# A gated delta-rule layer with a mixture of experts: the last chunk of each head no longer brings its state forward, and the first rows of x of the second output projection are asked for one step later

## The chip, the core and the metric

The kernel runs on one core of a Trainium2 chip. TensorE (PE) multiplies matrices, VectorE (DVE), ScalarE (ACT) and GpSimd (POOL) do the elementwise work, and SyncE (SP) issues most of the transfers between the chip's memory and the core. Each of them works through a queue of its own in order. The metric is the device time of one execution in microseconds (us), the median of several runs.

## The reference, cut to what matters

```python
xn = layernorm(x)                      # x: 2 x 2048 x 512, f32
q, k, v = silu(conv4(xn @ W))          # 16 heads of 128; the convolution runs over 4 tokens
alpha, beta = sigmoid(xn @ Wa + ba), sigmoid(xn @ Wb + bb)
def step(S, inps):                     # one token, one head; S starts at zero
    Sk = einsum('bhvk,bhk->bhv', S, kt)
    S = at * S - bt * ((Sk - vt) * kt) # the state, 128 x 128
    ot = einsum('bhvk,bhk->bhv', S, qt)
    return S, ot
_, o = scan(step, S0, ...)             # the last S is thrown away
attn = (layernorm(o) * ln_w + ln_b) * sigmoid(xn @ Wg) @ Wo
ffn = moe(first 512 tokens of xn)      # 16 experts, 4 per token
out = x + attn + ffn
```

Only the outputs `ot` are returned. The state that the scan ends with is used nowhere.

## The kernel before

**Tiling.** The tokens of a batch are cut into four blocks of 512 and each block into four chunks of 128, so there are 16 chunks (NC). The 16 heads of a batch are worked on two at a time (HG = 2): eight head pairs for each of the two batches, numbered u = 0 to 15. The token-by-token recurrence is done a chunk at a time with 128 x 128 matrices, and only the state S goes from a chunk to the next one of the same head pair, in the dictionary `state[u]`.

**One step of the recurrence.** `recurrence(b)` (L1118) goes over the 128 chunks of a batch. In a step it interleaves `before` of chunk m (operands that need no state: the decayed scores pT, the chunk's inverse matrix inv, k and v turned by the transposes L994 and L995, copied to `kv` at L1003, and `kg`, which is k times a decay, on POOL at L1009), `after` of chunk m - 1 (products with the state: L1041, r at L1045, w at L1052 and L1056, the state's update L1061 and L1068, the outputs L1076 and L1079) and `output` of chunk m - 2 (normalisation, gate, store of `oT` to oT_d at L1116). Among these stand the projections of the next block (`group`, seven half-size products in place of eight, L833), whose inputs `xr` come from xs_d by the loads of L812, the convolution's taps on DVE (L923), key work for later head pairs, the small triangular inverses on POOL (`inverses`, L268 and L271) and, in the first batch, the experts (L1754, L1771).

**What sets the order.** For PE, DVE, ACT and POOL the order is written out by hand: everything runs under `manual_schedule` for these four, and the generators yield at places that `recurrence` steps through. SP's queue is not written by hand. A scheduler with a simulated clock puts the transfers in order when the program is built. Transfers under `high_priority` are put ahead of others that are ready. A transfer on SP waits at the head of the queue until its buffer is free, its source is written and an older transfer on its semaphore has landed, and what stands behind it waits too.

**Buffers near the change.** `kg` has three buffers (the first output projection later keeps two pieces of weights in them), `S` and `kv` two each, the PSUM tag "c" (pq, pw, pss and the transposed output) two banks. `aTf` has two buffers. The keys' matrices go through them (`put_a`, stored to aT_d at L235), and in the second batch, after the last key, the first rows of x for the output projection.

**The output projections.** `out_pairs(b)` multiplies the gated outputs of two chunks at a time by Wo, again with seven products (L1336), and adds x. Before its first products it collects weights and inputs into buffers that the recurrence has finished with, by `stock`, `fetch_heads` and `get_x`, all through `load` (L1300), which is under `high_priority`. In the second batch `recurrence` steps it once in the last block but one (block n1 - 2, chunk 2), and then goes through it in the last four steps and behind them. The code ahead of its first yield runs in the first of these steps.

Of the kernel before, what the change touches and what calls it, by code (L numbers as in the profile page):

```python
# [8 lines left out]
F32 = mybir.dt.float32  # L9
# [7 lines left out]
P = 128  # L17
# [28 lines left out]
def block_kernel(ctx, tc, x, wq, wk, wv, wg, wo, wa, wb, ba, bb, par, consts,  # L46
# [11 lines left out]
    def bank(pool, tag):  # L58
        return pool.tile([P, 512], F32, tag=tag, name=tag)
# [705 lines left out]
    def bcast(a, n):  # L765
        return bass.AP(a.tensor, a.offset, [*a.ap, (0, n)])

    def v3(t):
        return t.rearrange("p (h j) -> p h j", h=HG)
# [187 lines left out]
    def before(n, c):  # L957

        u, blk = blocks[n]
        b = u // NP  # L960
        hs = slice((u % NP) * HG, (u % NP) * HG + HG)
        decs, kt, qt, _, vs, _ = have[n]
        op = ops[n % 2]
        ci, cs = blk * CB + c, slice(c * C, (c + 1) * C)

        inv = invs[(n * CB + c) % len(invs)]
        for g in range(2):
            nc.sync.dma_start(
                out=inv[g * Q:(g + 1) * Q, :, g * Q:(g + 1) * Q],
                in_=X_d[u][1, :, g, ci, :].rearrange("h (j i) -> j h i", i=Q))  # L970


        px = bank(ps_l, "l")
        nc.tensor.matmul(px[:, 0:Q], lhsT=op["a32"][:, c, :], rhs=op["ilo"][:, c, :],
                         start=True, stop=True)

        pk = bank(ps_l, "l")
        for h in range(HG):
            nc.tensor.matmul(pk[:, h * C:(h + 1) * C], lhsT=kt[:, h, cs], rhs=qt[:, h, cs],  # L979
                             start=True, stop=True)  # L980
        yield
        xs = k2.tile([P, Q], F32, tag="xs", name="xs")
        nc.vector.tensor_copy(xs, px[:, 0:Q])
        pT = k2.tile([P, HG, C], F32, tag="pT", name="pT", bufs=3)
        nc.vector.scalar_tensor_tensor(
            pT, v3(pk[:, 0:HW]), D ** -0.5, decs[:, :, c, 1:], ALU.mult, ALU.mult)
        yield

        pz = bank(ps_l, "l")
        nc.tensor.matmul(pz[:, 0:Q], lhsT=op["ihi"][:, c, :], rhs=xs, start=True, stop=True)  # L990

        pkv = bank(ps_l, "l")
        for h in range(HG):
            nc.tensor.transpose(pkv[:, h * D:(h + 1) * D], kt[:, h, cs], ident)  # L994
            nc.tensor.transpose(pkv[:, HW + h * D:HW + (h + 1) * D], vs[h][:, cs], ident)  # L995
        yield
        top, bot = op["top"][:, c, :], op["bot"][:, c, :]
        iT = k2.tile([P, Q], F32, tag="iT", name="iT")
        nc.vector.transpose(iT, pz[:, 0:Q])
        nc.vector.scalar_tensor_tensor(  # L1000
            top[:, 0:Q], pz[:, 0:Q], second[:, 0:1], top[:, 2 * Q:], ALU.mult, ALU.add)
        kv = k2.tile([P, 2, HG, D], F32, tag="kv", name="kv")
        nc.scalar.copy(kv.rearrange("p s h j -> p (s h j)"), pkv)  # L1003
        for h in range(HG):
            r = 64 * h
            nc.scalar.copy(bot[r:r + Q, r + Q:r + 2 * Q], iT[r:r + Q])  # L1006
            nc.gpsimd.tensor_copy(inv[0:Q, h, Q:2 * Q], iT[r + Q:r + 2 * Q])  # L1007
        kg = k2.tile([P, HG, D], F32, tag="kg", name="kg", bufs=3)
        nc.gpsimd.tensor_tensor(kg, kv[:, 0], bcast(gd1[b][:, ci, hs], D), ALU.mult)  # L1009
        yield  # L1010
        px = bank(ps_l, "l")
        nc.tensor.matmul(px[:, 0:C], lhsT=op["a64"][:, c, :], rhs=wide(top[:, 0:64]), start=True, stop=True)  # L1012
        yield
        xs = k2.tile([P, C], F32, tag="xs2", name="xs2")
        nc.scalar.copy(xs, px[:, 0:C])
        for h in range(HG):
            r = slice(64 * h, 64 * h + 64)
            nc.scalar.copy(inv[64:C, h, 64:C], bot[r, r])
        yield
        pz = bank(ps_l, "l")  # L1020
        nc.tensor.matmul(pz[:, 0:C], lhsT=xs, rhs=bot, start=True, stop=True)
        yield
        nc.scalar.copy(inv[0:64, :, 64:C], v3(pz[0:64, 0:C]))
        found[n, c] = (pT, kv, kg, inv)

    def after(n, c):

        u, blk = blocks[n]
        b = u // NP
        h0 = (u % NP) * HG  # L1030
        _, kt, _, qg, _, _ = have[n]
        pT, kv, kg, inv = found.pop((n, c))
        ci, cs = blk * CB + c, slice(c * C, (c + 1) * C)
        S = state.get(u)

        if S is None:
            r = kv[:, 1]
        else:
            pq = bank(ps_c, "c")
            for h in range(HG):  # L1040
                nc.tensor.matmul(pq[:, h * D:(h + 1) * D], lhsT=kt[:, h, cs], rhs=S[:, h, :],  # L1041
                                 start=True, stop=True)
            r = k2.tile([P, HG, D], F32, tag="r", name="r")
            for h in range(HG):
                nc.vector.scalar_tensor_tensor(  # L1045
                    r[:, h, :], pq[:, h * D:(h + 1) * D], gd0[b][:, ci, h0 + h:h0 + h + 1],
                    kv[:, 1, h, :], ALU.mult, ALU.add)
        yield
        yield
        pw = bank(ps_c, "c")  # L1050
        for h in range(HG):
            nc.tensor.matmul(pw[:, h * D:(h + 1) * D], lhsT=inv[:, h, :], rhs=r[:, h, :],  # L1052
                             start=True, stop=True)
        yield
        w = k2.tile([P, HG, D], F32, tag="w", name="w")
        nc.scalar.copy(w, v3(pw[:, 0:HW]))  # L1056
        yield

        pss = bank(ps_c, "c")
        for h in range(HG):  # L1060
            nc.tensor.matmul(pss[:, h * D:(h + 1) * D], lhsT=kg[:, h, :], rhs=w[:, h, :],  # L1061
                             start=True, stop=True)
        S2 = k2.tile([P, HG, D], F32, tag="S", name="S")
        if S is None:
            nc.vector.tensor_copy(S2, v3(pss[:, 0:HW]))
        else:
            for h in range(HG):
                nc.vector.scalar_tensor_tensor(  # L1068
                    S2[:, h, :], S[:, h, :], gtot[b][:, ci, h0 + h:h0 + h + 1],
                    pss[:, h * D:(h + 1) * D], ALU.mult, ALU.add)  # L1070
        state[u] = S2
        yield

        po = bank(ps_o, "o")
        for h in range(HG):
            nc.tensor.matmul(po[:, h * D:(h + 1) * D], lhsT=pT[:, h, :], rhs=w[:, h, :],  # L1076
                             start=True, stop=S is None)
            if S is not None:
                nc.tensor.matmul(po[:, h * D:(h + 1) * D], lhsT=qg[:, h, cs], rhs=S[:, h, :],  # L1079
                                 start=False, stop=True)  # L1080
        yield

        mv = k2.tile([P, HG, 2], F32, tag="mv", name="mv")
        for h in range(HG):
            st = k2.tile([P, 6], F32, tag="st", name="st")
            nc.vector.bn_stats(st, po[:, h * D:(h + 1) * D])
            nc.vector.bn_aggr(mv[:, h, :], st)
        rs = k2.tile([P, HG], F32, tag="rs", name="rs")
        nc.vector.tensor_scalar(rs, mv[:, :, 1], EPS, None, ALU.add)
        nb = k2.tile([P, HG], F32, tag="nb", name="nb")  # L1090
        nc.vector.tensor_scalar(nb, mv[:, :, 0], -1.0, None, ALU.mult)  # L1091
        nc.gpsimd.tensor_tensor(rs, rs, mhalf[:, 0:HG], ALU.pow)  # L1092
        nc.gpsimd.tensor_tensor(nb, nb, rs, ALU.mult)  # L1093
        outs[n, c] = (po, nb, rs)
# [197 lines left out]
    def out_pairs(b):  # L1292
# [63 lines left out]
        def get_x(i, m, n):  # L1356
            if whole[i % 2]:
                if n == 0:
                    c = 2 * order[i] + m
                    load(whole[i % 2][m], x[b, c * C:(c + 1) * C, :])  # L1360
                return
            load(xs[i % 2][m, n], x[of(i, m, n)])

        def rows(i, *tiles):
            for m, t in enumerate(tiles):
                whole[i][m] = t
                for n in range(2):
                    xs[i][m, n] = t[:, n * TH:(n + 1) * TH]
# [113 lines left out]
        else:  # L1482
# [12 lines left out]
            fetch_heads(a21, 0, 1, 0), fetch_heads(a22[0], 0, 1, 1)  # L1495
            for tag in ("wq", "wv"):
                stock("T2", bp.tile([P, 4 * TH], F32, tag=tag, name="wo", bufs=1), 4)
            rows(0, *(ap.tile([P, HID], F32, tag="aTf", name="xf", bufs=2) for _ in range(2)))
            for m in range(2):
                get_x(0, m, 0)  # L1500
            stock("T1", k2.tile([P, HID], F32, tag="act", name="wo", bufs=1), 2)
            for tag in ("swk", "swq"):
                stock("T1", k2.tile([P, 3 * TH], F32, tag=tag, name="wo", bufs=1), 3)
# [12 lines left out]
            both(s3, a11, a21, ALU.subtract)  # L1516
            e1 = snap(y, 1)
            yield
            rows(1, *(cvp.tile([P, HID], F32, tag="raw", name="xf") for _ in range(2)))
        def late():  # L1520
            while not last_done[0]:
# [316 lines left out]
```

## Time and profile before

| | before |
|---|---|
| median of 3 runs | 3581.33 us (3581.24 to 3588.71) |
| the profiled execution | 3581.82 us |
| its span | 3580.1 us |
| mean granted TensorE clock | 0.993 |
| first 230 us (norm, keys, routing): PE busy | 182.1 us |
| 230 to 1890 us (first batch): PE busy | 1634.7 of 1660 us |
| 1890 to 2090 us (first output projection): PE busy | 195.6 of 200 us |
| 2090 to 3440 us (second batch): PE busy | 1338.3 of 1350 us |
| 3440 us to the end (second projection): PE busy | 135.5 of 140.1 us |
| DMA engines' mean share, first batch / second batch | 0.75 to 0.77 / 0.63 |

Busy times are unions: matmuls that overlap are counted once. A step of one chunk takes 12.0 to 15.6 us in the first five head pairs, while the experts run too, and 10.2 to 11.1 us in most of the later ones. The span is the profiled execution from its first instruction to its last. The time of an execution is 1.7 us more.

### The profile page before, as it was taken

What the parts mean: (1) busy time and instruction counts of PE and PEld (TensorE: products, weight loads), DVE (VectorE), ACT (ScalarE), POOL (GpSimd) and SP (SyncE); (2) the same over time, 40 slices, a digit from 0 to 9 for tenths busy, and PEclk for the clock granted to TensorE, in tenths of its full rate; (3) what the DMA queues carried; (4) which work ended last, traced back from release to release, by engine and by line L of the source; (5) the groups of instructions that cost most, each with busy time, mean ns of one, the idle gap of its engine ahead of it and who ended that gap; (6) DMA issues with size and microseconds to landing.
All of it is one profiled execution on the core that took longest, in us unless ns stands there. A gap on an engine that the chain in (4) does not pass through costs nothing.

```text
span 3580.1 us, 69929 instructions
## 1 busy us (share of the span) xinstructions
PE 3486.3 (97%) x21588; PEld 3111.7 (87%) x21588; DVE 2568.2 (72%) x6467; ACT 2060.4 (58%) x5489; POOL 2119.9 (59%) x3680
## 2 busy tenths in 40 slices
PE   7889999999999999999999999999999999999999
PEld 4469889898988888898898889999999999899988
DVE  7877767677776767788784368888887888777532
ACT  4555656565655555676671047777777777666410
POOL 2147768687785867768661047676675758584300
PEclk9999999999999999999999999999999999999999
DMA  8777867768677686778787446575757575655432
GB/s 282 228 201 219 237 187 247 207 214 262 189 243 215 194 266 195 244 219 232 207 244 233 154 132 200 160 207 159 215 164 222 155 214 161 195 158 153 149 131 89
DMA packets 675107, 714.33 MB, mean 200 GB/s; under 512 B 364272, under 2 KB 468464, under 8 KB 674736
## 3 DMA queue, kind: packets, MB, share of 16 engines
q1 hardware_dynamic: 652624, 628.45, 59.6%
q0 software_dynamic: 22112, 81.41, 7.2%
q8 instruction: 175, 2.87, 0.3%
q14 instruction: 196, 1.61, 0.1%
HBM read 505.51 MB, written 204.08 MB: 198 GB/s over the span
## 4 chain that ended last, share of the span: by engine, by line
PE 84%; DMA 4%; DVE 2%; POOL 1%; issue 1%; ACT 1%; SPq 1%; POOLq 0%; DVEq 0%; ACTq 0%
PE y L833 22%; PE z L833 16%; PE z L1336 5%; PE p L1754 4%; PE l L979 3%; PE y L1336 3%; PE p L1336 3%; PE c L1061 3%; PE o L1076 3%; PE c L1052 3%; PE o L1079 3%; PE p L228 3%; PE c L1041 3%; PE p L1771 2%; DMA xr<-xs_d 2%; PE l L1012 2%
## 5 line engine op out<-in xcount | busy, mean ns | idle before, releaser
L923 DVE SCALAR_TENSOR_TENSOR cv<-raw,prm,cv 128x512 f32<-128x512 f32 x1086 | 944.9, 880 | 12.0 <-ACT cv L149 4.4
L1007 POOL COPY inv<-iT 32x32 f32<-32x32 f32 x512 | 197.6, 386 | 358.9 <-DVE top L1000 188.7
L1092 POOL TENSOR_TENSOR rs<-rs,mhalf 128x2 f32<-128x2 f32 x256 | 181.3, 708 | 378.6 <-DVE nb L1091 377.6
L838 ACT COPY e<-y 128x256 f32<-128x256 f32 x732 | 270.3, 369 | 221.4 <-PE y L833 214.4
L149 ACT ACTIVATE cv<-raw,prm 128x512 f32<-128x512 f32 x362 | 295.6, 817 | 108.3 <-DVE raw L899 108.2
L271 POOL TENSOR_TENSOR Y<-Y,t 128x30 f32<-128x30 f32 (+14 forms) x450 | 299.3, 665 | 35.3
L268 POOL TENSOR_TENSOR t<-Y 128x30 f32<-128x30 f32 (+14 forms) x450 | 281.5, 625 | 34.5 <-DMA inv<-X_d 22.0
L1068 DVE SCALAR_TENSOR_TENSOR S<-S,gtot,c 128x128 f32<-128x128 f32 x480 | 144.8, 343 | 178.1 <-PE c L1061 177.8
L899 DVE TENSOR_TENSOR raw<-z,e 128x256 f32<-128x256 f32 x244 | 103.4, 424 | 221.1 <-PE z L833 219.7
L1114 ACT ACTIVATE oT<-c,lnh 128x256 f32<-128x256 f32 x256 | 144.2, 563 | 185.2 <-PE c L1111 172.1
L1106 ACT ACTIVATE o<-o,nb,rs 128x128 f32<-128x128 f32 x512 | 202.4, 444 | 40.8 <-POOL nb L1093 39.7
L932 POOL TENSOR_TENSOR qg<-q,gin 128x512 f32<-128x512 f32 x126 | 183.0, 1453 | 68.2 <-DMA gin<-gin_d 51.3
L1115 POOL TENSOR_TENSOR oT<-g,oT 128x256 f32<-128x256 f32 x256 | 190.2, 743 | 23.3 <-ACT oT L1114 23.1
L833 PE MATMUL y<-xr,wq 128*128 128x256 f32 x744 | 192.9, 382 | 7.1 <-DMA xr<-xs_d 6.9
L833 PE MATMUL y<-xr,wg 128*128 128x256 f32 x756 | 195.2, 381 | 0.0
L1076 PE MATMUL o<-w,pT 128*128 128x128 f32 x1024 | 194.8, 274 | 0.0
L833 PE MATMUL y<-xr,wv 128*128 128x256 f32 x756 | 194.5, 380 | 0.0
L1079 PE MATMUL o<-S,qg 128*128 128x128 f32 x960 | 185.6, 275 | 0.0
L1754 PE MATMUL p<-xgT,w 128*128 128x128 f32 x1488 | 180.8, 275 | 4.9 <-DMA w<-in_ew,wrow 4.9
L1076 PEld LDWEIGHTS o<-w,pT 128*128 128x128 f32 x1024 | 173.1, 191 | 12.8
L1009 POOL TENSOR_TENSOR kg<-kv,gd 128x256 f32<-128x256 f32 x256 | 167.8, 655 | 25.4 <-ACT bot L1006 3.7
L855 DVE TENSOR_TENSOR raw<-z,e 128x256 f32<-128x256 f32 x244 | 102.4, 420 | 112.1 <-ACT e L838 43.5
(349 smaller groups left out, 10163.1 us busy)
## 6 DMA issues: line engine op xcount, KB each, us to landing
xr<-xs_d SPq DMA_DIRECT2D x189, 512.0 KB
row<-a_d SPq DMA_DIRECT2D x128, 258.0 KB
dec_d<-decA SPq DMA_DIRECT2D x128, 258.0 KB
decB<-dec_d SPq DMA_DIRECT2D x64, 516.0 KB
gin<-gin_d SPq DMA_DIRECT2D x128, 256.0 KB
k_d<-kf SPq DMA_DIRECT2D x128, 256.0 KB
k<-k_d SPq DMA_DIRECT2D x64, 512.0 KB
aT_d<-aTf SPq DMA_DIRECT2D x128, 256.0 KB
```

The lines of the kernel that those rows point to most:

```text
L149: nc.scalar.activation(cv, of, AF.Identity, bias=cbias(p, h0 + h), scale=tap(p, h0 + h, KS - 1))
L268: eng.tensor_tensor(t, bass.AP(col.tensor, col.offset, [col.ap[0], (Q, j), (0, n)]), bass.AP(row.tensor, row.offset, [row.ap[0], (0, j), ( ...
L271: eng.tensor_tensor(Y[:, 0:j, j + 1:], Y[:, 0:j, j + 1:], t, ALU.add)
L833: nc.tensor.matmul(ps[:, 0:TH], lhsT=a[i - 1][:, k, :], rhs=xs[j][:, slot, k, :], start=start and k == 0, stop=k == 1, skip_group_check=no ...
L838: nc.scalar.copy(e, py[:, 0:TH])
L923: nc.vector.scalar_tensor_tensor(cv, (r0, r1)[h][:, j:j + BLK], tap(p, u % NP * HG + h, j), cv, ALU.mult, ALU.add)
L1007: nc.gpsimd.tensor_copy(inv[0:Q, h, Q:2 * Q], iT[r + Q:r + 2 * Q])
L1076: nc.tensor.matmul(po[:, h * D:(h + 1) * D], lhsT=pT[:, h, :], rhs=w[:, h, :], start=True, stop=S is None)
L1079: nc.tensor.matmul(po[:, h * D:(h + 1) * D], lhsT=qg[:, h, cs], rhs=S[:, h, :], start=False, stop=True)
L1106: nc.scalar.activation(o[:, h, :], po[:, h * D:(h + 1) * D], AF.Identity, bias=nb[:, h:h + 1], scale=rs[:, h:h + 1])
L1336: nc.tensor.matmul(ps[:, 0:TH], lhsT=a[0][h // 4][:, h % 4, :], rhs=W[w][h], start=start and h == 0, stop=h == n8 - 1, skip_group_check=no ...
L1754: nc.tensor.matmul(ps[:fn, s, :], lhsT=w[f][:, s, k, :], rhs=xt[:, k, :], start=(k == 0), stop=(k == NKT - 1))
```

## The change

The last chunk of every head pair (`ci == NC - 1`) no longer computes what only the next chunk would need. In `before` the two transposes of k and the product `kg` go, and the copy to `kv` takes only v's half. In `after` the two products `pss` and the update into a new S go. This happens once for each of the 16 head pairs. Apart from that, in `out_pairs` for the second batch, the two tiles for the first rows of x and their loads move from ahead of the first yield to behind the first product's end, next to the tiles for the second rows.

```diff
@@ before
         pkv = bank(ps_l, "l")
+        last = ci == NC - 1
         for h in range(HG):
-            nc.tensor.transpose(pkv[:, h * D:(h + 1) * D], kt[:, h, cs], ident)
+            if not last:
+                nc.tensor.transpose(pkv[:, h * D:(h + 1) * D], kt[:, h, cs], ident)
             nc.tensor.transpose(pkv[:, HW + h * D:HW + (h + 1) * D], vs[h][:, cs], ident)
...
-        nc.scalar.copy(kv.rearrange("p s h j -> p (s h j)"), pkv)
+        if last:
+            nc.scalar.copy(kv[:, 1].rearrange("p h j -> p (h j)"), pkv[:, HW:2 * HW])
+        else:
+            nc.scalar.copy(kv.rearrange("p s h j -> p (s h j)"), pkv)
...
-        kg = k2.tile([P, HG, D], F32, tag="kg", name="kg", bufs=3)
-        nc.gpsimd.tensor_tensor(kg, kv[:, 0], bcast(gd1[b][:, ci, hs], D), ALU.mult)
+        kg = None
+        if not last:
+            kg = k2.tile([P, HG, D], F32, tag="kg", name="kg", bufs=3)
+            nc.gpsimd.tensor_tensor(kg, kv[:, 0], bcast(gd1[b][:, ci, hs], D), ALU.mult)
@@ after
-        pss = bank(ps_c, "c")
-        for h in range(HG):
-            nc.tensor.matmul(pss[:, h * D:(h + 1) * D], lhsT=kg[:, h, :], rhs=w[:, h, :],
-                             start=True, stop=True)
-        S2 = k2.tile([P, HG, D], F32, tag="S", name="S")
...
-        state[u] = S2
+        if kg is not None:
+            pss = bank(ps_c, "c")
...
+            state[u] = S2
         yield
@@ out_pairs, second batch
-            rows(0, *(ap.tile([P, HID], F32, tag="aTf", name="xf", bufs=2) for _ in range(2)))
-            for m in range(2):
-                get_x(0, m, 0)
             stock("T1", k2.tile([P, HID], F32, tag="act", name="wo", bufs=1), 2)
...
             yield from product(y, a11, "B11", True)
             both(s3, a11, a21, ALU.subtract)
             e1 = snap(y, 1)
             yield
+            rows(0, *(ap.tile([P, HID], F32, tag="aTf", name="xf", bufs=2) for _ in range(2)))
+            for m in range(2):
+                get_x(0, m, 0)
             rows(1, *(cvp.tile([P, HID], F32, tag="raw", name="xf") for _ in range(2)))
```

More of the change, by code (lines that the diff above doesn't have):

```diff
@@ L1057, in after @@
         yield
-        pss = bank(ps_c, "c")
-        for h in range(HG):
-            nc.tensor.matmul(pss[:, h * D:(h + 1) * D], lhsT=kg[:, h, :], rhs=w[:, h, :],
-                             start=True, stop=True)
-        S2 = k2.tile([P, HG, D], F32, tag="S", name="S")
-        if S is None:
-            nc.vector.tensor_copy(S2, v3(pss[:, 0:HW]))
-        else:
-            for h in range(HG):
-                nc.vector.scalar_tensor_tensor(
-                    S2[:, h, :], S[:, h, :], gtot[b][:, ci, h0 + h:h0 + h + 1],
-                    pss[:, h * D:(h + 1) * D], ALU.mult, ALU.add)
-        state[u] = S2
+        if kg is not None:
+            pss = bank(ps_c, "c")
+            for h in range(HG):
+                nc.tensor.matmul(pss[:, h * D:(h + 1) * D], lhsT=kg[:, h, :], rhs=w[:, h, :],
+                                 start=True, stop=True)
+            S2 = k2.tile([P, HG, D], F32, tag="S", name="S")
+            if S is None:
+                nc.vector.tensor_copy(S2, v3(pss[:, 0:HW]))
+            else:
+                for h in range(HG):
+                    nc.vector.scalar_tensor_tensor(
+                        S2[:, h, :], S[:, h, :], gtot[b][:, ci, h0 + h:h0 + h + 1],
+                        pss[:, h * D:(h + 1) * D], ALU.mult, ALU.add)
+            state[u] = S2
         yield
```

## The prediction

> **What bounds the kernel now.** I read the page first, then PE's table of waits, then timelines around the ends of the sixteen heads. (A "head" below is a head pair, numbered 0 to 15 over both batches.)
>
> ```profile
> span 3580.1 us, 69929 instructions
> ...
> PE 3486.3 (97%) x21588; PEld 3111.7 (87%) x21588; DVE 2568.2 (72%) x6467; ACT 2060.4 (58%) x5489; POOL 2119.9 (59%) x3680
> ```
>
> PE is busy for all but 93.8 us. Of its recorded idle time, 42.9 us lie ahead of 225 us, before the recurrence. In the recurrence and the projections PE's queue is the work itself, so a matmul taken out there is time taken out, unless a wait behind it grows by as much. The waits that could grow, from PE's table of waits (us in total, times, longest):
>
> ```profile
> PE y L833 <- DMA xr<-xs_d: 11.4, 9, 3.0
> ...
> PE c L1052 <- POOL inv L1007: 2.7, 1, 2.7
> ```
>
> Nine waits for a piece of x (xr) in 3.58 ms: loads mostly arrive in time, and where they don't they are the first suspects.
>
> **Part 1, the state at a head's end.** The last chunk's transposes and state products stand like this on PE. This is head 10, PE's timeline (start, us, operation):
>
> ```profile
> 2597.71 0.31 PE L990 MATMUL l<-xs,ihi 128*128 128x32 f32 x2
> 2597.85 0.30 PE L994 MATMUL l<-unit,k 128*128 128x128 f32 x1
> 2597.99 0.27 PE L995 MATMUL l<-unit,v 128*128 128x128 f32 x1
> 2598.10 0.27 PE L994 MATMUL l<-unit,k 128*128 128x128 f32 x1
> 2598.21 0.27 PE L995 MATMUL l<-unit,v 128*128 128x128 f32 x1
> 2598.32 1.03 PE L833 MATMUL y<-xr,swq 128*128 128x256 f32 x4
> ...
> 2600.27 0.61 PE L1061 MATMUL c<-w,kg 128*128 128x128 f32 x4
> 2600.72 1.06 PE L228 MATMUL p<-kf 128*128 128x128 f32 x8
> ```
>
> The durations overlap (0.27 us each, 0.11 us from start to start), so I price by starts. The two L994 go: 2 x 0.11 = 0.22 us (the first takes 0.14 only because it follows the narrow L990; its successor would inherit that). L1061 goes: 2600.72 - 2600.27 = 0.45 us. Together 0.67 us a head, and 16 x 0.67 = 10.7 us. Priced by durations instead (2 x 0.29 + 4 x 0.275 = 1.7 us a head) it would be 27 us; the starts rule that out.
>
> The other engines' share, with minimum/median/maximum ns:
>
> ```profile
> L1068 DVE SCALAR_TENSOR_TENSOR S<-S,gtot,c x480: 331/343/350, 258.3 to 3434.3; 128x128 f32<-128x128 f32 x160
> ...
> L1003 ACT COPY kv<-l x256: 583/586/614, 229.5 to 3415.2; 128x512 f32<-128x512 f32 x128
> L1009 POOL TENSOR_TENSOR kg<-kv,gd x256: 607/613/1150, 230.7 to 3415.9; 128x256 f32<-128x256 f32 x128
> ...
> L1056 ACT COPY w<-c x256: 350/372/379, 241.8 to 3430.2; 128x256 f32<-128x256 f32 x128
> ```
>
> DVE loses 2 x 0.343 x 16 = 11.0 us, POOL 0.613 x 16 = 9.8 us, and ACT's copy shrinks to the form of L1056: (0.586 - 0.372) x 16 = 3.4 us. I count all three at nothing: PE works throughout, and the waits of PE that end with one of these operations are L1012 on kv (1.3 us in the run) and none on S or kg of note. If that cover were gone it would be further gain, not loss. One fewer c bank, one fewer kg and S tile only make the next user's wait older. No wait is added on the four computing engines, whose order is otherwise the same.
>
> **What the waits give back.** Where PE waits for a load soon after the removed matmuls, it reaches the wait earlier and the load lands when it did. I looked at 45 us behind every head's end.
>
> ```profile
> 450.07 1.10 PE L833 MATMUL y<-xr,wq 128*128 128x256 f32 x4 [1.11 <-DMA xr<-xs_d]
> ...
> 455.42 1.10 PE L833 MATMUL y<-xr,wq 128*128 128x256 f32 x4 [1.16 <-DMA xr<-xs_d]
> ```
>
> Head 0: this load was issued at 440.90, ahead of the transposes (443.3) and of L1061 (447.5), so all 0.67 us turn into longer waiting. Heads 1 and 4: a wait for xr (0.47 us at 666.02, 0.98 us at 1325.92) stands between the transposes and L1061: 0.22 us lost in each. Head 13: 2.11 us for xr at 3116.79, issued in an unbroken row of SP issues: 0.67 us lost. Head 7 runs into the first output projection with gaps of 0.98, 1.40 and 1.08 us within 45 us, of which the last is a load: between 0 and 0.67 us lost, I take 0.33. The other eleven have no wait there, or one that follows PE's own earlier work. Sum 0.67 + 0.22 + 0.22 + 0.67 + 0.33 = 2.1 us, so 10.7 - 2.1 = 8.6 us remain.
>
> **SP's queue.** Its order isn't written by hand, and the shorter program gets another one. Placed side by side, the built queues hold the same transfers; at twelve head ends (0 to 6, 8 to 12) some operand loads (ilo, bot, top, ihi, a64, inv) move by up to five places against xr, k and oT_d; at two more, two neighbours swap. At heads 0 to 4 an xr comes one place earlier. Ahead of the first output projection two small loads of wo move nine to eleven places forward; their kg buffers were read long before, so they hold nobody up, and what they pass (q, decB) is used 18 us later. Bounds: one issue takes 0.43 us, so xr one place earlier is worth at most 5 x 0.43 = 2.2 us; the dearest late transfer in the trace is the POOL wait above (POOL itself waited 8.76 us for gin), 2.73 us of gap and about 1.7 us of slow clock after it. I take nothing, since the moved operands are needed a step (10 to 15 us) later.
>
> The clock rows, for that price (us; PE, PEld, DVE, ACT, POOL busy; PEclk, DMA share, GB/s):
>
> ```profile
> 1710.00:1712.50 2.50, 2.50 (x7) 1.97 (x7) 0.00 (x0) 0.69 (x2) 0.00 (x0) 0.50 0.92 307
> ...
> 3099.00:3102.00 3.00, 3.00 (x13) 2.76 (x13) 0.35 (x2) 1.53 (x5) 2.44 (x6) 0.50 0.72 161
> ...
> 3117.00:3120.00 3.00, 3.00 (x18) 2.72 (x18) 0.95 (x3) 1.12 (x3) 0.63 (x4) 1.00 0.52 129
> ```
>
> After gaps of 2.12 us (at 1709.6), 2.73 us (3098.6) and 3.04 us (1159.6) the granted clock was 0.50 for some 3.4 us, which costs half of that; after 2.11 us (3116.8) it stayed 1.00. Head 13's gap would grow to 2.78 us. So a drop could be added there and, with every gap moved by microseconds, one of the other three could vanish: -1.7 to +1.7 us, and I take 0. The Trainium skill, "TensorE: Matmul & The Clock Gate", section "HAM oscillation — how this bites in real kernels", gives the rule as no idle gaps above about 3.4 us; by that rule none of these gaps would cost clock, and the term would be 0 on both sides. The trace disagrees with it as a safe limit: three drops came after shorter gaps.
>
> **Part 2, the first rows of x of the second projection.** The step that asks for them is later, but SP's scheduler places a high-priority load where its buffer (aTf) comes free. In both built queues the two loads stand at the same places, 3582 and 3589, some 300 us ahead of their use, and moving them alone changes no queue at all. Cost and gain 0. So the second of them (issued 3097.05 after the queue had stood since about 3092.5, behind it gin and xr) still stands in front of the same transfers: the part doesn't do what it says.
>
> **The rivals.**
> - More is realised: no wait takes its share and xr comes earlier, 10.7 + 2.2 = 12.9 us, 3569. For it: eight heads (2, 6, 8 to 12, 15) show no PE wait at all behind the end. Against: the load in head 0 lay 9 us in flight with DMA 75% busy.
> - Loads eat it: if in the first batch's eight heads (DMA share 0.75 to 0.77) the slack of xr is under 0.67 us everywhere, only heads 8 to 15 pay, less head 13: 7 x 0.67 = 4.7 us, 3577, too little to be told from no change. For it: heads 0, 1, 4 and, ahead of its end, 6 do show xr waits; against: heads 2 and 5 show none, so their slack is unknown, not absent.
> - Slower: the new SP order lets a transfer come late at head ends, with PE gaps like that at 3098.61 and slow clock after each, 2.73 + 1.7 = 4.4 us apiece. Two such gaps eat the gain; four of the sixteen ends turn it into 4 x 4.4 - 8.6 = 9 us more, 3590. For it: SP is one queue and its head waits; against: places moved are few, and xr moves forward, not back.
>
> **How the numbers follow.** The profiled execution took 3581.82 us (span 3580.1 and 1.7 around it); the median of the runs is 3581.33. 3581.82 - 8.6 = 3573.2, against the median 3572.7: I say 3573. About 0.2% (7.2 us) can be told from no change here, so faster means under 3574.2. Forecast (3570.5 to 3575.5) 0.57, more realised 0.12, loads eat it 0.25, slower 0.06. Of the forecast's own chance 0.07 lies above 3574.2: faster 0.57 - 0.07 + 0.12 = 0.62, same 0.25 + 0.07 = 0.32, slower 0.06. The range goes from 3568.5 (more realised) to 3579 (loads eat it, plus a clock drop).
>
> **What would show it.** Right: L994 32 fewer instructions in the program, L1061 and the state updates likewise; the last chunk's L1012 followed by the next product 0.22 us later; a step at each head's end shorter by 0.67 us in heads 2, 8 to 12, 14, 15; PE's idle total up by about 2 us, at 450, 666, 1326 and 3117; the x rows still issued near 3080 to 3090. Wrong: steps shortened but PE's xr waits up by over 5 us, new gaps of PE behind head ends with PEclk 0.5, or the two rows of x issued some 300 us later than now.

## The result, and the profile after

The changed kernel takes 3577.94 us, the median of 18 runs (3566.68 to 3584.0). The kernel before took 3582.36 us in 18 runs beside them (3575.87 to 3597.59). The ratio is 0.9979 with a 95% interval of 0.997 to 0.9988, which is 7.5 us less (4.3 to 10.7). The means of the runs are 7.5 us apart, too, but the medians only 4.4. In a second measurement the ratio was 0.998 (0.9971 to 0.999).

A single profile cannot show this. Runs of one kernel differ by 10 us and more, and the profiled execution of the changed kernel is a long one: 3584.0 us against 3581.82 before. So below, a stage is compared over several profiles. The page after, its span and its busy time:

```profile
span 3582.2 us, 69674 instructions
...
PE 3484.2 (97%) x21492; PEld 3107.9 (87%) x21492; DVE 2554.3 (71%) x6435; ACT 2058.8 (57%) x5489; POOL 2109.5 (59%) x3664
```

PE has 96 fewer instructions (16 heads x 6), DVE 32, POOL 16. The three groups in which the update's work on DVE, ACT and POOL now stands (line, engine, operation, times, then busy us and mean ns):

```profile
L1016 POOL TENSOR_TENSOR kg<-kv,gd 128x256 f32<-128x256 f32 x240 | 156.8, 653 | 23.1 <-ACT bot L1011 2.4 <-issue 1.8
...
L1008 ACT COPY kv<-l 128x512 f32<-128x512 f32 x240 | 141.3, 589 | 46.7 <-PE l L997 42.4 <-issue 0.2
...
L1076 DVE SCALAR_TENSOR_TENSOR S<-S,gtot,c 128x128 f32<-128x128 f32 x448 | 135.4, 344 | 160.0 <-PE c L1069 159.8
```

These are 16, 16 and 32 fewer than before. (Line numbers have moved: L1061 is now L1069, L1052 is L1059, L994 and L995 are L996 and L997.) Head 10's end, PE's timeline (start, us, operation):

```profile
2590.98 0.31 PE L990 MATMUL l<-xs,ihi 128*128 128x32 f32 x2
2591.12 0.42 PE L997 MATMUL l<-unit,v 128*128 128x128 f32 x2
2591.38 1.03 PE L833 MATMUL y<-xr,swg 128*128 128x256 f32 x4
...
2600.54 0.61 PE L1059 MATMUL c<-r,inv 128*128 128x128 f32 x4
...
2603.33 0.38 PE L1019 MATMUL l<-top,a 128*128 128x128 f32 x2
2603.55 1.06 PE L228 MATMUL p<-kf 128*128 128x128 f32 x8
```

At 2591.12 only v's two transposes are left: 0.40 us from L990 to the next projection product, where a full set takes 0.61. At 2603.55 key work follows L1019 at once, where L1061 stood before. From L1059 to it are 3.01 us. Before, from the line below to the L228 of the prediction's fence at 2600.72, there were 3.46:

```profile
2597.26 0.61 PE L1052 MATMUL c<-r,inv 128*128 128x128 f32 x4
```

The gains are 0.21 and 0.45 us. (The L994 rows in the prediction's fence are those of head 11's first chunk, which share a step with head 10's last products. The last chunk's own stand a step earlier, at 2587.63, and cost the same: 0.61 us from L990 to the next projection product.)

The times of whole stages, from the start of a head's first w product to the next head's (us):

| profiles | heads 0 to 7 and first projection | heads 8 to 12, 14, 15 | head 13 |
|---|---|---|---|
| before | 1856.1 | 1161.2 | 171.5 |
| rows alone moved (same work) | 1859.9 | 1161.1 | 171.4 |
| after, two profiles | 1856.4, 1853.6 | 1157.1, 1157.3 | 173.3, 171.1 |

Head 15 is counted up to its last w product. In the second batch the gain is plain, 4.0 us with a scatter of some 0.3. In the first batch a gain of that size is hidden in the scatter: the same stage took 1867.1 us in a third kernel that brings every state of the first batch forward, and 1848.7 to 1864.0 in four more that don't at a head's end. Over these nine profiles the means are 1861.0 and 1855.6, 5.4 us apart, with a scatter of 5 us in each group.

### The profile page after: what moved, and what is told of

It reads as the page before. It is cut to its first block, busy times and chain, and to the rows that moved or that the text cites. A ratio compares the mean times of both kernels' runs of the same rounds, so it can differ in the third digit from the quotient of the medians.

```text
span 3582.2 us, 69674 instructions
## 1 busy us (share of the span) xinstructions
PE 3484.2 (97%) x21492; PEld 3107.9 (87%) x21492; DVE 2554.3 (71%) x6435; ACT 2058.8 (57%) x5489; POOL 2109.5 (59%) x3664
## 4 chain that ended last, share of the span: by engine, by line
PE 84%; DMA 4%; POOL 2%; DVE 2%; issue 1%; ACT 1%; SPq 0%; POOLq 0%; DVEq 0%; ACTq 0%
PE y L833 22%; PE z L833 16%; PE z L1344 5%; PE p L1762 4%; PE l L979 3%; PE p L1344 3%; PE y L1344 3%; PE o L1084 3%; PE c L1059 3%; PE c L1069 3%; PE p L228 3%; PE o L1087 3%; PE c L1048 3%; PE p L1779 2%; PE l L1019 2%; PE l L996 1%
## 5 line engine op out<-in xcount | busy, mean ns | idle before, releaser
L1012 POOL COPY inv<-iT 32x32 f32<-32x32 f32 x512 | 194.7, 380 | 362.3 <-DVE top L1002 188.2
L838 ACT COPY e<-y 128x256 f32<-128x256 f32 x732 | 270.3, 369 | 221.3 <-PE y L833 214.2
L1076 DVE SCALAR_TENSOR_TENSOR S<-S,gtot,c 128x128 f32<-128x128 f32 x448 | 135.4, 344 | 160.0 <-PE c L1069 159.8
L833 PE MATMUL y<-xr,wq 128*128 128x256 f32 x744 | 193.2, 382 | 11.6 <-DMA xr<-xs_d 11.0
L979 PE MATMUL l<-q,k 128*128 128x128 f32 x1024 | 177.6, 296 | 0.0
```

The costliest lines, as they stand in the source:

```text
L833: nc.tensor.matmul(ps[:, 0:TH], lhsT=a[i - 1][:, k, :], rhs=xs[j][:, slot, k, :], start=start and k == 0, stop=k == 1, skip_group_check=no ...
L838: nc.scalar.copy(e, py[:, 0:TH])
```

## The experiments

Each set was timed against runs of the kernel before on its own chip. Ratios are to that kernel, with 95% intervals.

**The second part alone.**

```diff
-            rows(0, *(ap.tile([P, HID], F32, tag="aTf", name="xf", bufs=2) for _ in range(2)))
-            for m in range(2):
-                get_x(0, m, 0)
...
             e1 = snap(y, 1)
             yield
+            rows(0, ...)   # the same three lines
```

> Part 2 alone: the first rows of x are asked for one step later in the program, and all state work stays. My theory: the built queues are the same as those of the kernel before, transfer for transfer, so ratio 1.000 to before, and any difference is the scatter of the measurement (medians of before alone moved from 3581.3 to 3582.4 us). Rival (the moved rows relieve SP's queue at the end of head 13, where PE waited 2.73 us and ran on slow clock after it): 2 to 4.4 us faster, ratio 0.9988 to 0.9994, and the load of the second row issued late in the trace.

Measured: 3589.41 us, 1.0001 (0.999 to 1.0013). The trace shows why: SP issues its 3989 transfers in the same order as in the kernel before. In the changed kernel, too, the rows (xf) are still asked for at head 13's end. The second one is issued 2.13 us after SP was done with the three transfers ahead of it (SP's timeline):

```profile
3091.81 1.72 SPq L259 DMA_DIRECT2D Y<-aT_d  x3
3095.66 0.35 SPq L1308 DMA_DIRECT2D xf<-in_x  x1
```

**The other engines' work put back.** The changed kernel with ACT's copy, POOL's product and DVE's update at their old sizes:

```diff
         if last:
-            nc.scalar.copy(kv[:, 1].rearrange("p h j -> p (h j)"), pkv[:, HW:2 * HW])
+            # both halves of kv written, from v's half read twice
...
+        kg = ...; nc.gpsimd.tensor_tensor(kg, kv[:, 0], ..., ALU.mult)   # always
...
+        else:   # last chunk: the update of S2, with pw in place of pss
```

> The change, with the work of the other engines put back at the last chunk: ScalarE copies 512 columns again (v's half twice), GpSimd multiplies a kg of the same size (from v's half), VectorE does two state updates of the same size (on the bank of w); nobody reads the results. Only TensorE's 2 transposes and 2 products per head stay away. My theory (TensorE's starts are the whole gain): as the changed kernel, ratio 0.998 to before, 7 to 8 us faster. Rival (the 11.0 us of VectorE, 9.8 us of GpSimd and 3.4 us of ScalarE carry the gain): ratio 1.000 to before.

Measured: 0.9989 (0.9978 to 0.9999). This lay between the two theories, so it was run again beside the changed kernel:

> The changed kernel with the work on ACT, POOL and DVE put back, once more, on the chip of the changed kernel: if the time of the change is PE's alone, its ratio to the changed kernel is 1.000 within 0.001; if the other engines' relief brings a part, 1.001 or more (3 us).

> The changed kernel once more, on the chip of the runs beside it: 0.998 of the kernel before (0.997 to 0.999), as measured. Its heads of the second batch should again be 0.45 to 0.67 us shorter each, and those of the first batch scatter by several us around the kernel before's.

Measured: 0.9985 (0.9977 to 0.9994) with the work put back, 0.998 (0.9971 to 0.999) without it. On the total the two can't be told apart. By stage they can: heads 8 to 12, 14 and 15 take 1157.3 and 1157.1 us with the work put back, exactly as the changed kernel's 1157.1 and 1157.3. In the second batch the gain is PE's alone. The first batch and its projection took 1861.4 and 1863.5 us with the work put back, and with SP's queue of that batch as in the changed kernel, against 1856.4 and 1853.6. So there the other engines may bring a part, but single profiles of one stage differ by as much: this stays open.

**Four chunks in place of one, in one batch.** The prediction's rival said that in the first batch loads take the gain. To see it above the scatter, the state is not brought forward in the last four chunks of heads 0 to 7, and in a second kernel of heads 8 to 15:

```diff
-        last = ci == NC - 1
+        last = ci >= NC - 4 and u < NP      # the second kernel: u >= NP
```

> The state is not brought forward in the last four chunks (instead of one) of heads 0 to 7, and heads 8 to 15 keep all of it: 32 chunks without transposes of k, kg, state products and update; those chunks use an older state, so the output is not the reference's. My theory: 32 x 0.67 = 21.4 us of TensorE's queue, less about 1.4 us given back at waits for loads in heads 0, 1, 4 and 7, so 20 us faster, ratio 0.9944. Rival (in the first batch the loads set the pace and eat it): under 7 us faster, ratio over 0.998, with TensorE's waits for xr up by over 10 us.

> The same in the last four chunks of heads 8 to 15 alone (the output is not the reference's). My theory: 32 x 0.67 = 21.4 us less 0.7 us at head 13, so 20.7 us faster, ratio 0.9942, as much as in the first batch. The rival (loads eat it in the first batch) expects the same here, about 21 us, so the two runs differ only by its claim. If the gain fails here too, the price of 0.67 us per chunk is wrong.

Measured: the first batch 0.9991 (0.9976 to 1.0006), 3 us less (2 more to 9 less); the second 0.9954 (0.9938 to 0.9971), 16.5 us less. One and the same edit is worth some five times as much in the second batch. There the eight heads went from 1332.8 to 1315.7 us, 0.53 us a chunk. That is less than 0.67, for a reason that the last chunk alone does not meet: in head 11 the first of the shortened steps kept its length, since the product behind the transposes (L1012, now L1019) started 2.94 us after the w product in both kernels, although the two transposes ahead of it were gone. Its operand `top` comes from DVE, which was in a scan of 1.66 us until shortly before, in both kernels. (With the four chunks of the second batch: w product at 2731.64 us, scan L219 from 2732.58, `top` at L1002 from 2734.27 for 0.20 us, L1019 at 2734.58.)

One place where the first batch's time went: PE's wait behind head 2's four chunks, and the stretches around it (us; PE, PEld, DVE, ACT, POOL busy; granted clock, DMA share, GB/s), of the first kernel:

```profile
896.99 2.05 PE L833 MATMUL y<-xr,wq 128*128 128x256 f32 x4 [3.52 <-DMA xr<-xs_d]
```

```profile
892.46:895.87 3.41, 1.01 (x10) 0.82 (x8) 0.30 (x2) 0.28 (x1) 2.83 (x5) 1.00 0.85 294
895.87:899.28 3.41, 2.29 (x6) 1.87 (x7) 0.00 (x0) 0.21 (x1) 0.79 (x1) 0.50 1.06 368
899.28:902.70 3.42, 3.42 (x13) 2.97 (x12) 1.16 (x4) 1.62 (x5) 1.13 (x4) 0.50 0.99 316
```

PE is early, the piece of x is not, the DMA engines' share is 0.85 to 1.06, and the clock is halved for 6.8 us after the gap. That head takes 221.3 us, more than before (217.6), with less to do.

**x loaded once.** To see whether it is the loads of x or something else, they are left out: in the first batch the pieces of x are loaded for one block and then kept. One kernel does only that, and the other has the four-chunk edit of heads 0 to 7 as well.

```diff
     def x_part(j, b, blk, where=None):
         lo, hi = PARTS[j]
+        if where is None and b == 0 and j in parts:
+            return
```

> The kernel before, with the pieces of x loaded only once in the first batch and then kept (the output is not the reference's): 28 blocks x 1.8 MB of loads go, no other instruction. It is the base for the next run. Both theories: PE's waits for xr in the first batch (9.1 us) and the slow clock behind them go, 10 to 15 us faster than the kernel before, 0.996 to 0.997.

> The run before, with the state not brought forward in the last four chunks of heads 0 to 7 (the output is not the reference's). Without x kept, the same edit gave 3 us of 20. Theory (in the first batch the time taken from PE comes back as waits for x): with x kept the edit pays as it did in the second batch, 0.52 us a chunk, 32 x 0.52 = 16.5 us less than the run before (0.9954 of it). Rival (something other than the loads of x sets the pace of the first batch: DVE, POOL, the experts' gathers, the keys' transfers): about 3 us less, 0.999 of the run before, with other waits in place of those for x.

Measured: 0.9956 (0.994 to 0.9972) and 0.9925 (0.9905 to 0.9944): 3568.55 and 3555.3 us. (The trace has 120 transfers fewer, the pieces of 30 blocks and not 28, and keeping x alone gave a little more than the 10 to 15 us expected.) With x kept the four chunks are worth 11 to 13 us, in heads 0 to 7 of the profiles 10.9 (1836.8 to 1825.9), where without it they were worth 3. The stretch of the first batch in the four kernels: before; four chunks; x kept; x kept and four chunks.

```profile
240.00:1890.00 1650.00, 1624.74 (x10631) 1473.84 (x10629) 1213.24 (x3025) 1011.61 (x2732) 1196.37 (x1985) 1.00 0.75 223
```

```profile
240.00:1890.00 1650.00, 1612.08 (x10439) 1457.31 (x10438) 1184.95 (x2962) 1005.20 (x2727) 1171.15 (x1955) 0.99 0.75 223
```

```profile
240.00:1890.00 1650.00, 1635.68 (x10720) 1485.45 (x10719) 1222.19 (x3050) 1016.35 (x2742) 1209.58 (x1991) 1.00 0.65 193
```

```profile
240.00:1890.00 1650.00, 1630.30 (x10576) 1475.65 (x10575) 1201.49 (x2991) 1010.60 (x2744) 1193.63 (x1961) 1.00 0.66 195
```

The DMA share is 0.75 without x kept and 0.65 with it. What becomes of the time taken from PE shows when the stretch from head 0's first w product to head 7's last one is split (us). "Work" is PE's busy time less half of the time at half clock, an estimate of what it would be at full clock:

| kernels | stretch | work | idle | at half clock | waits for xr |
|---|---|---|---|---|---|
| before | 1645.0 | 1616.3 | 25.3 | 6.8 | 9.1 |
| same work: rows alone moved | 1648.4 | 1616.5 | 28.5 | 6.8 | 10.2 |
| same work: four chunks of the second batch | 1654.7 | 1615.6 | 30.6 | 17.1 | 14.9 |
| four chunks of the first batch | 1646.5 | 1596.7 | 37.9 | 23.9 | 11.6 |
| x kept | 1627.0 | 1613.7 | 13.3 | 0 | 0 |
| x kept and four chunks | 1615.8 | 1595.1 | 17.3 | 6.8 | 0.3 |

Without x kept, 19.4 us of work go. 9.8 come back as idle time (against the mean of the first three rows) and 6.8 as slow clock (half of the 13.7 us more at half clock), so some 3 are left. With x kept 18.6 go, 4.0 and 3.4 come back, and 11.2 are left. So the theory holds for about two thirds of the 16.5 us. But the sign that the rival of the prediction had named, waits for xr up by over 10 us, did not come with the four chunks alone: 11.6 us lie within the 9.1 to 14.9 of the kernels without the edit. The idle time grew elsewhere, in waits for DVE's `raw` (6.6 us where the first three rows have 1.0 to 3.1) and in waits for which the profile names nothing (5.0, where they have 2.3 to 2.9). That the loads of x take most of the gain is shown by leaving them out. By which path they do it is not: with them gone, every other transfer has more room too. The rest went to waits that now come next. The two largest of PE's waits in the first batch of the last kernel are for ACT's `e` (5.0 us in 6 waits) and for DVE's `raw` (4.5 in 2).

**Head 13's end.** Here the changed kernel gains nothing in two profiles: 173.3 and 171.1 us, against 171.5 before. PE's timeline of the first one:

```profile
3111.59 1.10 PE L833 MATMUL y<-xr,wq 128*128 128x256 f32 x4 [1.45 <-DMA xr<-xs_d]
...
3117.34 2.04 PE L833 MATMUL y<-xr,wq 128*128 128x256 f32 x4 [3.32 <-DMA xr<-xs_d]
```

First the rows were really held, behind a store of oT:

```diff
-            for m in range(2):
-                get_x(0, m, 0)
+            with tc.issue_after(stored[0].ins):     # the last store of oT
+                for m in range(2):
+                    get_x(0, m, 0)
```

> The changed kernel, and the loads of the second projection's first two rows of x are really held: they may be issued only behind the last store of oT that the recurrence has issued by then, so that they stand some 330 places later in SP's queue (3919 and 3921 in place of 3582 and 3589). Theory (SP stands at head 13's end because the second row waits there for its buffer, and gin, xr and the small operands stand behind it): the stall of SP from 3093.5 to 3097 and PE's waits for xr behind it (1.45 and 3.32 us in the changed kernel) go, with the slow clock of 6.8 us that followed, so head 13 takes some 170.0 us in place of 173.3 and the kernel is 3 to 6 us faster than the changed one: 0.9965 to 0.997 of the kernel before. Rival (the waits at head 13's end come from the DMA engines, which then also load the projection's weights): the gap stays over 2 us and the time is that of the changed kernel, 0.998.

Measured: 0.9979 (0.9965 to 0.9992), the same as the changed kernel, as the rival had it. SP no longer stands for the second row, but xr is still late (PE's timeline). Head 13 took the 170.0 us that the theory had, but so it did in kernels that held nothing (169.4 to 173.7):

```profile
3121.72 1.18 PE L833 MATMUL y<-xr,wq 128*128 128x256 f32 x4 [2.94 <-DMA xr<-xs_d]
```

So SP's stall for the row was not the main cause. Next the weights of the projection's first segment were held too, with the same line around all the loads ahead of the first yield:

> As the run before, and all the loads of the second projection's first segment (weights and oT, 14 transfers of 256 to 512 KB) are held behind the same store. If the DMA engines' load by these weights is what makes xr late at head 13's end, this run loses the gap that the run with the rows alone keeps, and is 3 to 6 us faster than the changed kernel (0.9965 to 0.997). If SP's stall alone was the cause, it is equal to the run with the rows alone. If the weights then come late for the projection, it is slower at the end: PE waits for wo or for oT near 3440 us, over 5 us.

Measured: 0.9995 (0.9983 to 1.0006). Head 13 fell to 164.4 us, with no wait for xr, so the weights' transfers were the cause there. But in head 15 the product that reads them waited, with the DMA engines' share at 1.06, and the clock was halved for 6.8 us behind it. (The profile names no releaser for this wait. PE's next weight load waited 0.83 us for wo.)

```profile
3353.46 4.23 PE L1346 MATMUL y<-wo,o 128*128 128x256 f32 x8 [5.04 <-issue]
```

Head 15 rose from 163.9 to 171.2 us, so the 3 to 6 us hoped for didn't come. Then the same loads behind a store in the middle of head 14:

```diff
+        if u == 2 * NP - 2 and ci == 6:
+            stored[0] = kept_store
```

> The changed kernel, with the two rows of x and the first segment's weights and oT held behind the store of oT of head 14's seventh chunk, so that they stand some 90 to 100 places of oT's stores earlier than in the run that held them all into head 15, and behind head 13's end. Theory (those loads cost head 13's end its waits for xr and its slow clock; held into head 15 they came too late there, a wait of 5.04 us and 6.8 us of slow clock): head 13 as with all held (164.4 us against 173.3 in the changed kernel), head 15 as in the changed kernel (163.9): 6 to 9 us faster than the changed kernel, 0.9955 to 0.9965 of the kernel before. Rival (any place for these 5 MB costs as much): heads 13 to 15 together as long as in the changed kernel (481.2 us), 0.998.

Measured: 0.9986 (0.9976 to 0.9996). Head 13 took 164.9 us, but head 14 rose from 144.0 to 150.5, with another wait in place of that for xr:

```profile
3208.30 1.22 PE L1059 MATMUL c<-r,inv 128*128 128x128 f32 x4 [3.59 <-POOL inv L1012]
```

POOL was late with inv because it had stood for gin, a load that SP issued at 3199.62, behind thirteen of the held loads in a row (POOL's timeline):

```profile
3205.72 1.26 POOL L932 TENSOR_TENSOR qg<-q,gin 128x512 f32<-128x512 f32 x1 [7.49 <-DMA gin<-gin_d]
```

The rival held: in one piece these loads cost about the same in the three places tried. Heads 13 to 15 took 479.7 and 479.1 us in these two, 481.2 and 478.9 in the changed kernel. So at last each load got a store of its own to stand behind:

```diff
+        if (u == 2 * NP - 2 and ci >= 2) or (u == 2 * NP - 1 and ci < 4):
+            held.append(kept_store)
...
-            with tc.high_priority():
+            with tc.high_priority(), tc.issue_after(held.pop(0).ins) if held else ExitStack():
                 return nc.sync.dma_start(out=to, in_=src)
```

> The changed kernel, and the loads of the second projection's first segment each held behind a store of oT of its own, one for each chunk from head 14's third chunk on, instead of being issued together at head 13's end. Theory (together they delay whatever stands behind them: xr at head 13's end, inv's pieces in head 14, wo itself in head 15; one at a time they fit into the DMA engines' free time): head 13 at 164.5 to 165, head 14 at 144.0, head 15 at 163.8 us, together 472.5 against 481.2 in the changed kernel and 479.1 to 479.7 where they were held in one piece; so 6 to 9 us faster than the changed kernel: 0.9955 to 0.9965 of the kernel before. Rival (the loads cost the same time wherever they are): heads 13 to 15 together 477 or more, 0.998.

Measured: 3574.05 us, 0.997 (0.9956 to 0.9985), some 11 us less than the kernel before, and by its ratio the shortest of the kernels that compute the whole layer. The ratio lies between the theory's and the rival's, and its interval takes in both and overlaps that of the changed kernel. So the stages have to decide: heads 13, 14 and 15 took 166.0, 144.1 and 164.3 us, together 474.4. In the five profiles with the head's end shortened and the weights not held, they took 477.3 to 481.2. That is one profile of this kernel, but it speaks for the theory. One wait for xr is left at head 13's end:

```profile
3108.24 1.10 PE L833 MATMUL y<-xr,wq 128*128 128x256 f32 x4 [1.28 <-DMA xr<-xs_d]
```

## Why the prediction was right in its total, and where its steps failed

The forecast was 3573 us, 8.6 less than before by its own sum. Measured were 7.5 less (4.3 to 10.7) by the means of the runs, and 4.4 by the medians. So the change is about the one forecast, and the median of 3577.94 us lies in the range given (3568.5 to 3579). But it lies above the forecast's own band of 3570.5 to 3575.5, and within 1 us of the 3577 of the rival "loads eat it". One reason is that the median of the kernel before was 1 us higher in these runs than in the three that I had. The total alone doesn't tell the two stories apart, and the way to it holds in part.

**The price of a head's end (0.67 us): right.** 0.45 us at the product and 0.21 at the transposes in head 10. In head 11 the last two full steps went from 10.23 and 10.67 us to 10.01 and 10.22 (the same in the second profile). Seven heads of the second batch give 7 x 0.67 less the last product of head 15, which lies behind the stretch measured: 4.2 forecast, 4.0 found. In the first batch the price holds for the work, if not for the time: in the split used above, the six profiles with only the last chunk's work gone have 1611.5 us of work in the mean, where the first three rows have 1616.1. That is 4.7 less, for eight pairs of transposes and seven products, 4.9 by the price. Pricing by starts and not by durations (27 us in all) was what made the size right.

**ACT, POOL and DVE at nothing: right in the second batch,** by the kernels with their work put back. It isn't settled in the first.

**What the waits give back ("the other eleven have no wait there"): the step that failed.** I read single waits of one profile as fixed places and took back 2.1 us. Done the same way for four chunks of the first batch, this gives back 1.4 of 21.4 us. In the split above 16.6 of 19.4 came back, 9.8 as idle time of PE and 6.8 as slow clock. The waits don't keep their places or lengths either. In the two profiles of after, with one program and one queue, those for xr in the first batch stand at 892, 1110 and 1715 us, and at eight places from 281 to 1850 us, none of them at 450 or 1326, where I expected more idle time. In the kernel with the rows alone moved, which has the queue of before, four of five are near places of before (666, 1160, 1326 and 1715), but last 1.15, 2.13, 2.10 and 3.17 us in place of 0.47, 3.04, 0.98 and 2.12, and head 0, where I took away 0.67, has none.

I also misread two heads. The transposes at 443.3 in head 0 belong to head 1's first chunk; its own last ones stand at 430.8, ahead of the load's issue at 440.90, so by my rule only the product's 0.45 us were lost. And head 6's wait of 2.12 us, at 1707.5, stands between its transposes (1699.4) and its product (1716.0), so by the same rule it loses 0.22. The two cancel out in the sum.

Was the rival right, then? Its price, 4.7 us for the second batch alone, is about what the second batch gave: 4.0 us, 0.45 for head 15's last product, and head 13 between 0.4 us shorter and 1.8 longer. What the total of 7.5 has beyond this, some 3 to 5 us by difference, would be the first batch's, out of 8 x 0.67 = 5.4. The means of the nine profiles say 5.4, with a scatter as large. The run with four chunks (3 us) speaks for a smaller share, some 1 us, and the interval of the total (4.3 to 10.7 us) takes in either. So how much of the first batch's 5.4 us a single chunk keeps isn't settled. That four chunks keep little of theirs is.

**Head 13: right in kind.** Its longest wait grew from 2.11 us to 3.32 and 2.38 us in the two profiles of after, where I had 2.78. It also had 6.8 and 3.4 us at half clock, where before had 3.4, so the drop that I had as a possibility came in the first profile.

**Clock drops as 0 ± 1.7 us: the rule behind it was wrong.** I went by the length of a gap and had 2.11 us without a drop beside 2.12 with one, and left it. The section on the hardware below shows what decides. The size was too narrow too: from 260 us to the last projection the time at half clock was 10.2 us before and 20.4 and 13.6 after, which costs half of the difference, 5.1 and 1.7 us. Such differences come without the change, too: two other kernels with the first batch's work of before had 6.8 and 20.5.

**SP's new order at 0.** No profile of the change shows a new late operand at a head's end in the second batch. The order alone was not tried.

**The second part without effect: right,** 1.0001.

## What to carry to other kernels

Work taken out of an engine that is busy 97% of the time pays only where the transfers that it waits for have room. In this kernel the same edit was worth 0.5 us a chunk in a batch with a DMA share of 0.63 and 0.1 in one with 0.75, and there 0.35 once the loads of x were left out and the share was 0.65. Split a stage into work, idle time and slow clock: here the work of six profiles lies within 1.3 us, where the time of their first batch differs by 15. A wait that one profile shows is one draw of several, so a stage is judged by its sum over several profiles, or by an edit made four times as large. A block of loads that was late in each of three places was cured by spreading it, not by moving it.

## What the runs showed of the hardware

The clock is not set by the length of a gap. In the fourteen profiles of this case, between 260 and 3440 us, all changes of the clock fall on a grid of 3.41 us, and they go with how busy PE was within one cell of it. Before, the gap of 2.12 us that was followed by a drop, and the one of 2.11 us that was not, cut at the grid:

```profile
1706.07:1709.48 3.41, 1.41 (x12) 1.20 (x10) 1.85 (x6) 2.87 (x8) 1.64 (x4) 1.00 0.86 239
1709.48:1712.90 3.42, 3.30 (x8) 2.71 (x9) 0.00 (x0) 0.69 (x2) 0.00 (x0) 0.50 0.88 278
3112.36:3115.77 3.41, 2.32 (x18) 2.03 (x16) 2.12 (x9) 1.56 (x5) 0.22 (x1) 1.00 0.68 163
3115.77:3119.19 3.42, 2.40 (x14) 2.22 (x15) 0.40 (x2) 0.37 (x1) 1.35 (x3) 1.00 0.80 244
```

The first gap lies in one cell, with PE busy for 1.41 of 3.41 us, and the next cell is at half clock. The second is shared by two cells, 2.32 and 2.40 us busy, and nothing follows. After, the gap at head 13's end grew to 3.32 us:

```profile
3112.64:3116.06 3.42, 1.38 (x13) 1.19 (x11) 1.51 (x7) 1.08 (x3) 1.09 (x3) 1.00 0.71 203
3116.06:3119.47 3.41, 2.13 (x5) 1.80 (x6) 0.00 (x0) 0.05 (x1) 0.47 (x1) 0.50 0.84 195
```

In these profiles all 47 drops follow a cell in which PE was busy for 0 to 0.48 of the time. Of some 12,900 cells at full clock with no drop behind them, none lies under 0.44. A drop lasted one cell where PE was busy for 0.82 of that cell or more, and two where it was busy for 0.34 to 0.83 of it. The Trainium skill, "TensorE: Matmul & The Clock Gate", section "HAM oscillation — how this bites in real kernels", has no gaps above about 3.4 us as its rule. The grid's length agrees with that figure. As a safe limit for a gap it doesn't hold here, since 2.12 us in the wrong place were enough.
